# Layer 0 of a four-layer hybrid on one core: the step size and C are kept by chunk in memory, and the sums of the four directions are added there

## The chip, the core and the metric

One core of a Trainium2 chip runs the whole network in one launch. Its engines run side by side, each through its own list of instructions in order: TensorE (PE, with its weight loads shown as PEld), VectorE (DVE), ScalarE (ACT), GpSimd (POOL) and SyncE (SP, which here only issues transfers). They wait for each other through semaphores. The metric is the device time of one execution in microseconds, as the median of repeated runs.

## The reference

The input is 4 images of 64 x 64 positions with 128 channels. The change touches layer 0 alone, a selective scan over 256 inner channels and 16 states, in four directions (along rows, along columns, and both backwards):

```python
xz = x @ w_in
xc, z = jnp.split(xz, 2, axis=-1)
xc = conv_general_dilated(xc, conv_w, ...) + conv_b          # 3 x 3, by channel
xa = jax.nn.silu(xc)
x_flat = xa.reshape(b, L, D_INNER)                           # L = 4096
dts, Bp, Cp = jnp.split(x_flat @ w_xproj, [DT_RANK, DT_RANK + D_STATE], axis=-1)
dts = dts @ w_dt
xs = jnp.stack([x_flat, x_t, jnp.flip(x_flat, 1), jnp.flip(x_t, 1)], axis=1)

def step(h, inp):                                            # 4096 steps, every direction
    u_i, d_i, b_i, c_i = inp                                 # d_i = softplus(dts + b_dt)
    dA = jnp.exp(d_i[..., None] * A)
    h = h * dA + (d_i * u_i)[..., None] * b_i[:, None, :]
    y = jnp.einsum('gdn,gn->gd', h, c_i)
    return (h, y)

y = (the four directions, each put back in place, added) + 4 * xa * D
y = layer_norm(y) * silu(z);   x = x + y @ w_out
```

delta, B and C are the same in all four directions: they follow the scan's own time, and only u differs. Layers 1 to 3 are not changed.

## The kernel before

**Units and iterations.** A unit is one image b and one half h of the 256 channels. A unit is 64 chunks c of 64 time steps, so layer 0 is one loop of 4 x 2 x 64 = 512 iterations, I = (2b + h) * 64 + c. An iteration handles the four directions of its chunk as two pairs: kp = 0 along rows (forward j = 0, backward j = 1) and kp = 1 along columns. Partitions hold 64 channels (or times) for two groups of states; 16 states are two groups of 8.

**What an iteration does**, with lines of the profile:

- `fetch` (SP) loads for iteration I + 2: C broadcast over partitions (`ct`, L570), u of the four directions with time on partitions (`xo`, L583), and, for h = 1, the diagonals of B (`dg`, L588). `load` loads delta for four chunks (`dl` L536, `dp` L539).
- `start` copies delta's chunk backwards (`dlr`, ACT, L599); `diagonal` makes diagonals of B (ACT, L608, 16 instructions, h = 0 only) and stores them (L611); `decay` makes exp(delta A) for the next four chunks (ACT, L560).
- `delta` turns delta's chunk so that time stands on partitions, forwards in one half and backwards in the other (PE, L617, into the PSUM tile `aux`); `inputs` multiplies it with u into `du`, two DVE instructions (L628), one for each pair.
- `products`: PE multiplies du with the diagonals (L637) and so makes delta u B with channels on partitions again, in PSUM.
- `scan`: for each direction DVE adds the state carried over into the first column (L650) and scans 1024 columns (L653). POOL then makes the carry for the next chunk (`cy`, L661) and multiplies the states by C in place (`big`, L669, one for each pair).
- `total`: PE adds the 8 states of a group and both groups (L682, 16 matmuls in two parts). In the second half of a unit (c >= 32) the four places of `yr` and `yc` hold the sums of the opposite direction, and PE adds these in by identity matmuls (L694). ACT copies the sums into `yr` (rows) or `yc` (columns), L701. Both tiles are whole (128 x 4096) and single. yr is stored by SP (L706) in the second half, yc is added to y0 in memory by a POOL transfer (L710) at the end of a unit.

**Order.** PE, DVE and ACT run in the order written out in the loop; Tile's scheduler places POOL's and SP's instructions. In iteration I the loop writes: start(I + 1), diagonal(I + 1), products(I, 0), scan(I, 0), total(I - 2, 1), a side step, decay, products(I, 1), delta(I + 1), inputs(I + 1), scan(I, 1), a side step, total(I - 1, 0). The states lie in three buffers, the products' PSUM in three.

**Side steps.** A generator `beside` is advanced twice an iteration, one step each time, from c = 4 of h = 0 on. For image 0 it runs `spectra` (tables for layer 1, lines 814 to 872), for later ones `back` of the image before: y = yr + y0 (POOL, L468), layer norm (L475 to L497), the product with silu(z) (POOL, L501), w_out (L508, L512) and the store. Then `front` of the next image (group norm, w_in: L281, L328) and, from h = 1 on, `middle`: convolution (L369), silu, turning of u into memory `xT` (L387, L391), w_xproj (L402), B turned (L417), and softplus for both halves (ACT L435 to L440, DVE L442 to L446) with delta stored to `dl`. front and middle of image 0 run ahead of the loop, back of the last image after it.

Of the kernel before, what the change touches and what calls it, by code (L numbers as in the profile page):

```python
# [14 lines left out]
P = 128  # L15
# [144 lines left out]
def layer0(cm, x, W, x1, also, kept):  # L160
# [5 lines left out]
    with ExitStack() as ctx:  # L166
# [4 lines left out]
        t4 = ctx.enter_context(tc.tile_pool(name="l0t4", bufs=4))  # L171
        p2 = ctx.enter_context(tc.tile_pool(name="l0p2", bufs=2))
# [32 lines left out]

        both = tl(wp, [P, TC], "both")
# [27 lines left out]

        yr = tl(wp, [P, S], "yr")
        yc = tl(wp, [P, S], "yc")

        aux = tl(pp, [P, 2, 2, P], "aux")
        yp = aux[:, 0].rearrange("p k (j t) -> p k j t", t=TC)
        pt2 = aux[:, 1]  # L240
# [19 lines left out]
        def begin(b):  # L260
            img[b] = {
                "zs": tl(dr, [P, 2, S], "zs"),
                "dl": tl(dr, [2, P, S], "dl_d"),
                "ct": tl(dr, [NST, S], "ct_d"),
                "xT": tl(dr, [2, S, P], "xT_d"),
                "y0": tl(dr, [P, 2, S], "y0_d"),
                "yr": tl(dr, [P, 2, S], "yr_d"),
            }
# [77 lines left out]
        def shifted(i, pool, tag):  # L346

            k, h = divmod(i, 2)
            x3 = tl(pool, [3 * CG, 4, 8 * PADW], tag, bufs=None if tag == "big" else 1)
            for dy in range(3):  # L350
                s0 = (8 * k + dy) * PADW
                nc.sync.dma_start(
                    x3[dy * CG : (dy + 1) * CG],
                    xc_d[4 * h : 4 * h + 4, :, s0 : s0 + 8 * PADW].rearrange("g p s -> p g s"),
                )
            return x3

        def middle(b, bank, pool, tag, ahead):

            ready = [shifted(i, pool, tag) for i in range(ahead)]  # L360
            for k in range(NBLK):
                cols = slice(k * BLK, (k + 1) * BLK)
                xa = []
                for h in range(2):
                    ps = bank()
                    x3 = ready.pop(0)
                    for dx in range(3):
                        for g in range(4):
                            nc.tensor.matmul(  # L369
                                ps[g * CG : (g + 1) * CG, :], lhsT=cdiag[:, 4 * h + g, dx, :],  # L370
                                rhs=x3[:, g, 0 : 8 * PADW].rearrange(
                                    "p (r w) -> p r w", w=PADW
                                )[:, :, dx : dx + HW],
                                start=(dx == 0), stop=(dx == 2),
                            )
                    if 2 * k + h + ahead < 2 * NBLK:
                        ready.append(shifted(2 * k + h + ahead, pool, tag))
                    xh = tl(tmp, [P, BLK], "t2k")
                    nc.scalar.activation(xh, ps, AF.Silu, bias=vec[:, 0, h : h + 1])
                    y0 = tl(tmp, [P, BLK], "t2k")  # L380
                    nc.scalar.activation(y0, xh, AF.Copy, scale=d4[:, h : h + 1])
                    nc.sync.dma_start(img[b]["y0"][:, h, cols], y0)
                    xa.append(xh)
                    yield
                    ps = bank()
                    for i in range(4):
                        nc.tensor.transpose(  # L387
                            ps[:, i * P : (i + 1) * P], xa[h][:, i * P : (i + 1) * P], cm.ident
                        )
                    t = tl(tmp, [P, 4, P], "t2k")  # L390
                    nc.scalar.copy(t, ps.rearrange("p (t c) -> p t c", c=P))  # L391
                    nc.sync.dma_start(
                        img[b]["xT"][h, cols, :].rearrange("(t p) c -> p t c", p=P), t
                    )
                    yield
                    if h == 0:
                        yield
                        yield
# [12 lines left out]
                nc.sync.dma_start(img[b]["ct"][:, cols], xd[RANK + NST : n, :])  # L411
# [10 lines left out]
                nc.vector.tensor_copy(BT[:, 8 * k : 8 * k + 8, :], pb)  # L422
                for h in range(2):
# [23 lines left out]
                    nc.sync.dma_start(img[b]["dl"][h, :, cols], r)  # L447
                yield

# [81 lines left out]
        def load(q):  # L531

            b, h, c = place(q * QC)
            cols = slice(c * TC, (c + QC) * TC)
            dl = tl(p2, [P, QC * TC], "dl")
            nc.sync.dma_start(dl, img[b]["dl"][h, :, cols])  # L536
            dp = tl(p2, [P, 2, QC, TC], "dp")
            for p in range(2):
                nc.sync.dma_start(  # L539
                    dp[p * TC : (p + 1) * TC].rearrange("p g c t -> p g (c t)"),  # L540
                    img[b]["dl"][h, :, cols].rearrange("(g d) t -> d g t", d=TC),
                )
            return {"dl": dl, "dp": dp, "dA": dA[q % 2], "h": h}
# [21 lines left out]
        def fetch(I):  # L565
# [3 lines left out]
            for p in range(2):  # L569
                nc.sync.dma_start(  # L570
                    ct[p * TC : (p + 1) * TC],
                    img[b]["ct"][p * NH0 : (p + 1) * NH0, c * TC : (c + 1) * TC]
                    .unsqueeze(0).to_broadcast([TC, NH0, TC]),
                )
            xo = tl(p2, [P, 2, P], "xo", bufs=3)
            xT = img[b]["xT"][h]
# [12 lines left out]
            inp[I] = {"ct": ct, "xo": xo, "dg": dg}  # L589
# [4 lines left out]
        def start(I):  # L594
            b, h, c = place(I)
            q = {"c": c, "h": h, "w": quads[I // QC], **inp.pop(I)}
            dlc = q["w"]["dl"][:, c % QC * TC : (c % QC + 1) * TC]
            dlr = tl(p2, [P, TC], "dlr")
            nc.scalar.copy(dlr, dlc[:, ::-1])  # L599
            q["dl"] = dlc, dlr  # L600
            return q
# [11 lines left out]
        def delta(q):  # L613

            pt = pt2[:, q["c"] % 2]
            for j in range(2):
                nc.tensor.matmul(  # L617
                    pt[j * TC : (j + 1) * TC, :], lhsT=q["dl"][j], rhs=cm.ident,
                    start=True, stop=True,
                )  # L620
            q["pt"] = pt

        def inputs(q):

            q["du"] = []
            for kp in range(2):
                d_ = tl(p2, [P, P], f"du{kp}")
                nc.vector.tensor_tensor(d_, q["xo"][:, kp, :], q["pt"], ALU.mult)  # L628
                q["du"].append(d_)

        def products(q, kp):
            bs = [tl(db, [P, 2 * NH0, TC], "db") for _ in range(2)]
            for g in range(2):
                for j in range(2):
                    half = slice(j * TC, (j + 1) * TC)
                    for p in range(2):
                        nc.tensor.matmul(  # L637
                            bs[j][p * TC : (p + 1) * TC, g * NH0 : (g + 1) * NH0, :],
                            lhsT=q["du"][kp][half, g * TC : (g + 1) * TC],
# [5 lines left out]
        def scan(I, q, kp, bs, st, old, new):  # L645
            c = q["c"]
            for j in range(2):
# [11 lines left out]
            us = slice(2 * kp, 2 * kp + 2)  # L659
# [16 lines left out]
        def total(I, part):  # L676
            b, h, c = place(I)
            st = states[I]
            late = c >= NCHUNK // 2
            for n in range(4 * part, 4 * part + 4):  # L680
                for p in range(2):
                    nc.tensor.matmul(  # L682
                        yp[p * TC : (p + 1) * TC], lhsT=both,
                        rhs=st[:, :, p * NH0 + n, :], start=(n == 0),
                        stop=(n == NH0 - 1 and not late),
                    )
            if part == 0:
                return
            vs = [views(yc if kp else yr, c)[2 * j + kp] for j in range(2) for kp in range(2)]
            for j in range(2 if late else 0):  # L690

                for kp in range(2):
                    v = vs[2 * j + kp]
                    nc.tensor.matmul(  # L694
                        yp[:, kp, j, :], lhsT=cm.ident, rhs=v[:, ::-1] if j else v,
                        start=False, stop=(j + kp == 2),
                    )
# [5 lines left out]
            if late and c % 8 == 7:  # L703
                for r in (c - 7, NCHUNK - 1 - c):
                    rows = slice(r * TC, (r + 8) * TC)
                    nc.sync.dma_start(img[b]["yr"][:, h, rows], yr[:, rows])  # L706
            if c == NCHUNK - 1:
                for r in range(2):
                    rows = slice(r * S // 2, (r + 1) * S // 2)
                    nc.gpsimd.dma_start(  # L710
                        img[b]["y0"][:, h, rows], yc[:, rows], accum_op=ALU.add
# [12 lines left out]
        for _ in run(front(0, turn_bank), middle(0, turn_bank, big, "big", 2)):  # L724
            pass
        N = 2 * B * NCHUNK
        states, quads, inp = {}, {0: load(0), 1: load(1)}, {}
# [9 lines left out]
        delta(nxt)  # L737
# [10 lines left out]
        with tc.manual_schedule(engines=engines):  # L748
            for I in range(N):
                b, h, c = place(I)  # L750
                clock[0] = I
                if h == 0 and c == 4:
                    gens = [back(b - 1, own_bank) if b else also(
                        tl(p2, [P, 4, 8 * PADW], "x3", bufs=1)[:, 0, 0 : 4 * C], tmp, t4, own_bank
                    )]
                    if b + 1 < B:
                        gens += [
                            front(b + 1, own_bank), wait(I - c + NCHUNK),
                            middle(b + 1, own_bank, p2, "x3", 1),
# [22 lines left out]
                if I > 1:  # L782
                    total(I - 2, 1)
# [10 lines left out]
                if nxt:  # L794
                    delta(nxt)
# [4 lines left out]
                if I:  # L800
                    total(I - 1, 0)
                carry = new
            total(N - 2, 1)
            total(N - 1, 0)
            total(N - 1, 1)
# [4 lines left out]
def spectra(cm, W, cst, sp_d, room, tmp, t4, bank):  # L810

    nc = cm.nc
    kern = room.rearrange("p (a c) -> p a c", c=C)
# [1504 lines left out]
```

## Time and profile before

| | |
|---|---|
| median of 3 runs | 11002.33 us (10992.38 to 11011.69) |
| the profiled execution, time and span | 10974.05 us and 10972.3 us |
| busy over the span: PE, DVE, ACT, POOL | 86%, 69%, 49%, 49% |
| the 512 iterations (first to last scan) | 281.7 to 6370.9 us |
| units of h = 0 (b = 0 to 3) | 762.9, 810.7, 807.2, 790.8 us |
| units of h = 1 (b = 0 to 3) | 747.2, 746.1, 750.4, 673.9 us |
| granted TensorE clock in the units | 0.92 to 0.99 |

A group line reads: line, engine, operation, out<-in, shapes, count | busy us, mean ns of one | idle time of the engine just before them, and what ended most of it. A waits line reads: who waited <- for whom: total us, times, longest. A timeline line reads: start us, duration us, engine, line, operation, out<-in, shapes, how many merged, and in brackets the idle time before it and its releaser. The third table row and the unit rows come from one answer of the windows view.

### The profile page before, as it was taken

What the parts mean: (1) busy time and instruction counts of PE and PEld (TensorE: products, weight loads), DVE (VectorE), ACT (ScalarE), POOL (GpSimd) and SP (SyncE); (2) the same over time, 40 slices, a digit from 0 to 9 for tenths busy, and PEclk for the clock granted to TensorE, in tenths of its full rate; (3) what the DMA queues carried; (4) which work ended last, traced back from release to release, by engine and by line L of the source; (5) the groups of instructions that cost most, each with busy time, mean ns of one, the idle gap of its engine ahead of it and who ended that gap; (6) DMA issues with size and microseconds to landing.
All of it is one profiled execution on the core that took longest, in us unless ns stands there. A gap on an engine that the chain in (4) does not pass through costs nothing. (4 is left out here: it accounts for less than half of the span.)

```text
span 10972.3 us, 163387 instructions
## 1 busy us (share of the span) xinstructions
PE 9474.1 (86%) x59368; PEld 4529.1 (41%) x59368; DVE 7569.2 (69%) x11174; ACT 5425.1 (49%) x13536; POOL 5331.9 (49%) x2581
## 2 busy tenths in 40 slices
PE   6789998889998899998889954999999956988886
PEld 2344444344443344443344432444444434544442
DVE  1898988888988898988899966545452122355546
ACT  6666543555544564545542223777776622433321
POOL 0788888878888888887889940000000000000000
PEclk7899999999999899998999977999999976677777
DMA  5334443334443334443333341111100065022101
GB/s 147 106 107 149 131 128 114 109 109 149 136 132 116 107 117 151 135 122 113 109 106 99 103 120 36 41 35 35 39 24 17 16 191 104 17 46 56 37 24 46
DMA packets 1471160, 1009.46 MB, mean 92 GB/s; under 512 B 697540, under 2 KB 1296296, under 8 KB 1466008
## 3 DMA queue, kind: packets, MB, share of 16 engines
q1 hardware_dynamic: 1468056, 982.24, 30.3%
q0 software_dynamic: 2304, 16.78, 0.7%
q8 instruction: 475, 7.78, 0.3%
q14 instruction: 325, 2.66, 0.1%
HBM read 667.01 MB, written 331.61 MB: 91 GB/s over the span
## 5 line engine op out<-in xcount | busy, mean ns | idle before, releaser
L653 DVE TENSOR_TENSOR_SCAN big<-dA,db 128x1024 f32<-128x1024 f32 x2048 | 4680.0, 2286 | 82.1 <-ACT dA L560 3.2
L669 POOL TENSOR_TENSOR big<-big,ct 128x2048 f32<-128x2048 f32 x1024 | 4646.1, 4537 | 85.0 <-DVE big L653 5.4
L637 PE MATMUL db<-dg,du 64*64 64x512 f32 x16384 | 2442.7, 617 | 101.1 <-DVE db L650 87.8
L682 PE MATMUL aux<-big,both 128*64 128x256 f32 x16384 | 2104.0, 401 | 407.1 <-DVE db L650 260.6
L682 PEld LDWEIGHTS aux<-big,both 128*64 128x64 f32 x16384 | 1202.8, 142 | 1396.1 <-issue 622.9
L701 ACT COPY yr<-aux 128x64 f32<-128x64 f32 x1024 | 226.6, 222 | 2668.6 <-PE aux L694 1250.7
L637 PEld LDWEIGHTS db<-dg,du 64*64 64x64 f32 x16384 | 748.2, 135 | 1321.2 <-issue 1218.4
L608 ACT ACTIVATE dg<-mask,BT 128x64 f32<-128x64 f32 x4096 | 1007.4, 341 | 4.0 <-DMA dg_d<-dg 4.0
L1441 PE MATMUL av<-e,x 128*128 128x512 f32 x2048 | 974.0, 592 | 4.6 <-ACT e L1436 4.6
L1392 PE MATMUL qk<-a,xT 128*128 128x512 f32 x2048 | 966.6, 594 | 8.6 <-ACT e L1396 7.8
L1396 ACT ACTIVATE e<-qk,nk 128x512 f32<-128x512 f32 x1024 | 692.9, 685 | 539.2 <-PE qk L1392 538.4
L560 ACT ACTIVATE dA<-dp,A 128x252 f32<-128x252 f32 x2048 | 870.5, 509 | 1.4
L971 POOL TENSOR_TENSOR g_rs<-g_rs,qrow 128x4 f32<-128x4 f32 x32 | 41.1, 1285 | 1499.9 <-DVE g_rs L970 1499.9
L661 POOL TENSOR_TENSOR cy<-big,a 128x32 f32<-128x32 f32 x1008 | 272.8, 271 | 821.7 <-DVE big L653 524.4
L1392 PEld LDWEIGHTS qk<-a,xT 128*128 128x128 f32 x2048 | 378.0, 190 | 462.3 <-issue 358.0
L1441 PEld LDWEIGHTS av<-e,x 128*128 128x128 f32 x2048 | 381.6, 190 | 434.7 <-issue 393.6
L1436 ACT ACTIVATE e<-e 128x1024 f32<-128x1024 f32 x510 | 538.7, 1056 | 15.3
L1917 ACT ACTIVATE e<-s 72x576 f32<-72x576 f32 x448 | 273.3, 642 | 492.0 <-PE s L1910 489.0
L628 DVE TENSOR_TENSOR du<-xo,aux 128x128 f32<-128x128 f32 x1024 | 248.2, 284 | 379.5 <-PE aux L617 286.2
L650 DVE TENSOR_TENSOR db<-db,cy 128x16 f32<-128x16 f32 x2016 | 336.9, 167 | 202.0 <-PE db L637 184.2
L1928 POOL COPY vp<-vt 72x160 f32<-72x160 f32 x56 | 19.6, 352 | 890.8 <-PE po L1934 874.4
L2150 DVE SCALAR_TENSOR_TENSOR tex<-x,gw,tex 128x128 f32<-128x128 f32 x768 | 264.5, 344 | 256.1 <-PE x L2144 241.2
(525 smaller groups left out, 10869.4 us busy)
## 6 DMA issues: line engine op xcount, KB each, us to landing
ct<-ct_d SPq DMA_DIRECT2D x1024, 128.0 KB
dg_d<-dg SPq DMA_DIRECT2D x256, 512.0 KB
dg<-dg_d SPq DMA_DIRECT2D x256, 512.0 KB
xo<-xT_d SPq DMA_DIRECT2D x2048, 32.0 KB
x<-xc_d SPq DMA_DIRECT2D x144, 264.0 KB
dp<-dl_d SPq DMA_DIRECT2D x256, 128.0 KB
t2k<-in_x SPq DMA_DIRECT2D x96, 256.0 KB
sp<-sp_d SPq DMA_DIRECT2D x16, 1280.0 KB
```

The lines of the kernel that those rows point to most:

```text
L560: nc.scalar.activation(w["dA"][:, :, g, n, 1:], w["dp"][:, g, :, 1:], AF.Exp, scale=A[:, w["h"], g, n : n + 1],)
L608: nc.scalar.activation(q["dg"][:, n, :], mask, AF.Copy, scale=BT[:, q["c"], n : n + 1])
L637: nc.tensor.matmul(bs[j][p * TC : (p + 1) * TC, g * NH0 : (g + 1) * NH0, :], lhsT=q["du"][kp][half, g * TC : (g + 1) * TC], rhs=q["dg"][ha ...
L650: nc.vector.tensor_tensor(bs[j][:, :, 0], bs[j][:, :, 0], old[:, u, :], ALU.add)
L653: nc.vector.tensor_tensor_scan(st[:, u].rearrange("p n t -> p (n t)"), q["w"]["dA"][:, c % QC].rearrange("p g n t -> p (g n t)"), bs[j].re ...
L669: nc.gpsimd.tensor_tensor(sv, sv, q["ct"].rearrange("p n t -> p (n t)").unsqueeze(1) .to_broadcast([P, 4, NH0 * TC]), ALU.mult,)
L682: nc.tensor.matmul(yp[p * TC : (p + 1) * TC], lhsT=both, rhs=st[:, :, p * NH0 + n, :], start=(n == 0), stop=(n == NH0 - 1 and not late),)
L1392: nc.tensor.matmul(ps, lhsT=me["xT"][:, kt * P : (kt + 1) * P], rhs=me["a"][k], start=True, stop=True,)
L1396: nc.scalar.activation(e[:, j, :], ps, AF.Exp, bias=me["nk"][:, kt : kt + 1], scale=2.0)
L1436: nc.scalar.activation(es[g + 2], es[g + 2], AF.Exp)
L1441: nc.tensor.matmul(avs[b, k], lhsT=img[b]["x"][:, kt, :], rhs=e[:, j, :], start=(kt == 0), stop=(kt == NT - 1),)
L1917: nc.scalar.activation(e.rearrange("p j h q -> p j (h q)"), ss[p][0:HALF, :, 0 : 2 * WIN], AF.Exp, scale=0.5,)
```

## The change

- middle: once softplus is done for both halves, delta is turned (PE, then ACT), its halves reversed by a matmul with `flip`, copied again and stored in memory by chunk (`dT`): eight stores a block of 512 positions. C is stored by chunk, so that a chunk's eight states lie in one piece.
- The loop loads the turned delta (`dt`) in fetch, and `du` becomes one DVE instruction over both pairs. delta(), dlr and the dl load go.
- The sums go into tiles of 8 chunks (`yr0`, `yr1`) and of half a unit (`yc`), two of each. The identity matmuls go. yr is stored by SP in a unit's first half and added in memory by POOL transfers in its second; yc is added in memory twice a unit.
- Both parts of total work on I - 2: part 0 after scan(I, 0), part 1 at the end. A third side step is taken at c % 4 == 2 of h = 0; beside starts at c = 5; the idle steps in middle go. The convolution's input is loaded in two halves from the pool of `t4k` tiles, and spectra's kernels lie in `padded[0]`.

```diff
+        flip = tl(wp, [P, P], "flip")
+        nc.vector.memset(flip, 0.0)
+        for p in range(2):
+            half = slice(p * TC, (p + 1) * TC)
+            nc.vector.tensor_copy(flip[half, half], cm.ident[half, half][:, ::-1])
...
-        yr = tl(wp, [P, S], "yr")
-        yc = tl(wp, [P, S], "yc")
...
-                "ct": tl(dr, [NST, S], "ct_d"),
+                "ct": tl(dr, [NCHUNK, NST, TC], "ct_d"),
+                "dT": tl(dr, [2, NCHUNK, 2, TC, P], "dT_d"),
...
-            x3 = tl(pool, [3 * CG, 4, 8 * PADW], tag, bufs=None if tag == "big" else 1)
+            x3 = [tl(pool, [3 * CG, 2, 8 * PADW], tag) for _ in range(2)]
...
-                    if h == 0:
-                        yield
-                        yield
...
                     nc.sync.dma_start(img[b]["dl"][h, :, cols], r)
-                yield
+                    rs.append(r)
+
+                yield
+                for h in range(2):
+                    t = None
+                    for j in range(2):
+                        ps = bank()
+                        if j == 0:
+                            for i in range(4):
+                                nc.tensor.transpose(
+                                    ps[:, i * P : (i + 1) * P], rs[h][:, i * P : (i + 1) * P],
+                                    cm.ident,
+                                )
+                        else:
+                            nc.tensor.matmul(
+                                ps, lhsT=flip, rhs=t.rearrange("p t c -> p (t c)"),
+                                start=True, stop=True,
+                            )
+                        t = tl(tmp, [P, 4, P], "t2k")
+                        nc.scalar.copy(t, ps.rearrange("p (t c) -> p t c", c=P))
+                        for i in range(2):
+                            nc.sync.dma_start(
+                                img[b]["dT"][h, 8 * k + i : 8 * k + 8 : 2, j]
+                                .rearrange("t r c -> r t c"), t[i * TC : (i + 1) * TC],
+                            )
+                        yield
...
+            dt = tl(p2, [P, P], "dt", bufs=3)
+            nc.sync.dma_start(dt, img[b]["dT"][h, c].rearrange("j r c -> (j r) c"))
...
         def inputs(q):
 
-            q["du"] = []
-            for kp in range(2):
-                d_ = tl(p2, [P, P], f"du{kp}")
-                nc.vector.tensor_tensor(d_, q["xo"][:, kp, :], q["pt"], ALU.mult)
-                q["du"].append(d_)
+            q["du"] = tl(p2, [P, 2, P], "du")
+            nc.vector.tensor_tensor(
+                q["du"], q["xo"], q["dt"].unsqueeze(1).to_broadcast([P, 2, P]), ALU.mult
+            )
...
+                if c % 8 == 0:
+                    for i in range(2):
+                        ys[i] = tl(yb, [P, 8 * TC], f"yr{i}")
+                if c % (NCHUNK // 2) == 0:
+                    ys[2] = tl(yb, [P, HW, TC], "yc")
...
-            for j in range(2 if late else 0):
-
-                for kp in range(2):
-                    v = vs[2 * j + kp]
-                    nc.tensor.matmul(
-                        yp[:, kp, j, :], lhsT=cm.ident, rhs=v[:, ::-1] if j else v,
-                        start=False, stop=(j + kp == 2),
-                    )
...
+                for i, r0 in enumerate((c - 7, NCHUNK - 1 - c)):
+                    to = img[b]["yr"][:, h, r0 * TC : (r0 + 8) * TC]
+                    if c < NCHUNK // 2:
+                        nc.sync.dma_start(to, ys[i])
+                    else:
+                        nc.gpsimd.dma_start(to, ys[i], accum_op=ALU.add)
-            if c == NCHUNK - 1:
+            if c % (NCHUNK // 2) == NCHUNK // 2 - 1:
                 for r in range(2):
                     rows = slice(r * S // 2, (r + 1) * S // 2)
                     nc.gpsimd.dma_start(
-                        img[b]["y0"][:, h, rows], yc[:, rows], accum_op=ALU.add
+                        img[b]["y0"][:, h, rows],
+                        ys[2].rearrange("p r w -> p (r w)")[:, rows], accum_op=ALU.add,
                     )
...
-                if h == 0 and c == 4:
+                if h == 0 and c == 5:
...
                 scan(I, now, 0, bs, st, carry, new)
                 if I > 1:
-                    total(I - 2, 1)
+                    total(I - 2, 0)
                 if beside:
                     next(beside, None)
...
                 bs = products(now, 1)
                 if nxt:
-                    delta(nxt)
                     inputs(nxt)
                 scan(I, now, 1, bs, st, carry, new)
                 if beside:
                     next(beside, None)
-                if I:
-                    total(I - 1, 0)
+                if I > 1:
+                    total(I - 2, 1)
+                if beside and h == 0 and c % 4 == 2:
+                    next(beside, None)
                 carry = new
```

## The prediction

> **What bounds the kernel now.** I read first the page's digits in 40 slices and its list of costliest groups. Layer 0 takes the first 23 slices, and there DVE, PE and POOL are all busy eight or nine tenths. The first two groups are the scan on DVE and the product with C on POOL:
>
> ```profile
> L653 DVE TENSOR_TENSOR_SCAN big<-dA,db 128x1024 f32<-128x1024 f32 x2048 | 4680.0, 2286 | 82.1 <-ACT dA L560 3.2
> L669 POOL TENSOR_TENSOR big<-big,ct 128x2048 f32<-128x2048 f32 x1024 | 4646.1, 4537 | 85.0 <-DVE big L653 5.4
> ...
> L628 DVE TENSOR_TENSOR du<-xo,aux 128x128 f32<-128x128 f32 x1024 | 248.2, 284 | 379.5 <-PE aux L617 286.2
> L650 DVE TENSOR_TENSOR db<-db,cy 128x16 f32<-128x16 f32 x2016 | 336.9, 167 | 202.0 <-PE db L637 184.2
> ```
>
> Second, the windows by unit (64 iterations). The 512 iterations run from 281.7 to 6370.9 us: 6089.2, of which DVE is busy 5422.5, PE 5445.6, POOL 5073.8 and ACT 3063.3. So DVE idles 667, and the two rows above say before what: du waits for TensorE's turned delta, and the carry (L650) for the products.
>
> Third, the waits view of that window, for causes:
>
> ```profile
> POOL cy L661 <- DVE big L653: 524.4, 342, 17.6
> DVE du L628 <- PE aux L617: 286.2, 265, 15.1
> ...
> DVE db L650 <- PE db L637: 184.2, 62, 17.9
> ...
> POOL t4k L468 <- DMA t4k<-yr_d: 80.4, 15, 10.4
> ACT yr L701 <- DMA yr_d<-yr: 69.7, 6, 21.0
> ```
>
> POOL waits for DVE, so DVE leads; the last row is the single yr tile that is still being stored when the next unit writes it.
>
> Fourth, the timeline of a plain iteration (start, duration):
>
> ```profile
> 6013.84 2.29 DVE L653 TENSOR_TENSOR_SCAN big<-dA,db 128x1024 f32<-128x1024 f32 x1
> ...
> 6016.24 0.27 POOL L661 TENSOR_TENSOR cy<-big,a 128x32 f32<-128x32 f32 x1
> 6016.28 0.48 DVE L628 TENSOR_TENSOR du<-xo,aux 128x128 f32<-128x128 f32 x2 [0.15 <-DMA xo<-xT_d]
> ...
> 6016.59 4.53 POOL L669 TENSOR_TENSOR big<-big,ct 128x2048 f32<-128x2048 f32 x1
> 6016.68 0.18 DVE L650 TENSOR_TENSOR db<-db,cy 128x16 f32<-128x16 f32 x1
> 6016.89 2.29 DVE L653 TENSOR_TENSOR_SCAN big<-dA,db 128x1024 f32<-128x1024 f32 x1
> ```
>
> Scan follows scan after 2.40 us, but after 3.05 with du between: du costs 0.65, and the iteration 10.25.
>
> Fifth, a long stall of the output part (back), and a DVE instruction that met POOL:
>
> ```profile
> 2227.46 2.34 POOL L468 TENSOR_TENSOR t4k<-t4k 128x1024 f32<-128x1024 f32 x1 [6.49 <-PE aux L617]
> ...
> 2234.65 3.68 PE L682 MATMUL aux<-big,both 128*64 128x256 f32 x16 [7.36 <-POOL big L669]
> ...
> 2241.22 0.18 DVE L650 TENSOR_TENSOR db<-db,cy 128x16 f32<-128x16 f32 x1 [6.26 <-PE db L637]
> ```
>
> ```profile
> 481.70 4.51 POOL L669 TENSOR_TENSOR big<-big,ct 128x2048 f32<-128x2048 f32 x1
> 482.95 3.54 DVE L862 SCALAR_TENSOR_TENSOR t4k<-t4k 128x256 f32<-128x256 f32 x1
> 486.41 0.17 DVE L650 TENSOR_TENSOR db<-db,cy 128x16 f32<-128x16 f32 x1
> ```
>
> The first: POOL is late by one add, the sums of iteration I-1 wait for it, the products stand behind them on PE, and DVE pays 6.3. The second: L862 reads two SBUF tiles, starts 1.25 into a POOL product and ends 0.28 after it, 3.54 us for what L856, of the same size, does in 0.42 (median).
>
> **What DVE must still do.** du becomes one instruction of 256 columns from two SBUF tiles. Nearest row: L856, 0.40 us, the next instruction 0.32 later (521.25 to 521.57). I take 0.33 for 0.65. 512 x (4 x 2.40 + 0.33) = 5084. The side work on DVE in the loop is unchanged: reciprocals 94, softplus 99, back 77 (L480, L494, L512), spectra's other four 41 (L856, L862, L865, L868), statistics and copies 26, together 338 with rounding. Together 5422.
>
> **What goes from the waits.** du no longer follows TensorE, so the 286 us, and most of the other 93 before L628, go: PE drops the turning (0.45 us an iteration) and, in late iterations, four identity adds (0.8). Sums of I-2 instead of I-1 give POOL half an iteration more, so the 6.3 us stalls of back go. Double yr and yc tiles take the wait at c = 2 away. The copy dlr (0.24 of ACT each) and the dl load go; both were off the path.
>
> **What stays or comes**, in us:
> - The wait for spectra's kernels at 372.95 (17.9) and the first scan's 3.2: 21, untouched.
> - Start of back, three images. Iterations c = 2 and 4 took 24.1 and 19.1, that is 23 above plain. POOL's add still waits for y0 and yr, now both accumulated by POOL's DMA (14.2 to landing), but the carries alone then hold DVE: 11 each, 33. Bounds 0 and 69.
> - A convolution step is 2.78 on PE (133.6/48). With products and sums, 1.95 each, its half takes 6.7 against DVE's 4.8; PE is some 1.5 ahead: 0.4 x 48 = 19. Bounds 0 and 1.9 each (91).
> - The input part (front) puts 1.0 of PE into a step (four of 105.7/96 and one of 31.6/48, by five), at 2.25 steps an iteration with the third ones: 7.8 + 2.3 = 10.1 against 9.93. Some 78 iterations (30 of image 0, 24 each of 1 and 2, counted in the program's order) x 0.3 = 23; bounds 0 and 70.
> - du against POOL. POOL's pair cy and product repeats every 4.82, two make 9.65, with the a0 products (0.5 in four iterations) and du's hold (cy took 0.40 behind L856 at 388.38, 0.27 elsewhere) about 9.9. So du arrives when POOL's product is just ending. In iterations without DVE side work 0.2 x 290 = 58. What makes POOL later is no longer absorbed but paid at the next du: 24 adds L468 of 2.35, 55; 48 pairs of accumulating DMAs instead of 8 (1.76 a pair at 1811.49), of which DVE's side work hides a third, 55. In all 168. Lower bound nothing, if a tensor_tensor isn't held; upper bound half a product at each du, 2.27 x 512 = 1162. I take 168 because the rate of POOL (9.9) and DVE (9.93) keeps du at the product's end.
> - SP gains a dt load an iteration (xo's loads take 0.6 each), dT stores and twice as many convolution loads. In the plain iteration above it issues for 1.28 (ct), 0.57 (dg) and 5.84 (xo), 7.7 of 10.25, and loads are 1.5 iterations ahead: 15 for late ones (xo cost 22.4 so far). Bounds 0 and 45.
>
> Together 279; the loop becomes 5701, 388 less.
>
> The turns themselves in the loop (48 x 2 halves: four transposes 0.66, a 512-column matmul 1.1, two copies 0.58) lie in steps of their own on PE and ACT, under DVE. The third steps, the dropped idle ones and the start at c = 5 only place them; x3 in halves from another pool and the kernels' new room move buffers. I count nothing for these; uncovered, a turn step is a PE step of 1.1, less than a convolution's 2.8.
>
> **Before the loop** they are not hidden. In the program's order PE turns all of a block's delta before the next block's convolution, which now runs beside the softplus. From the last logarithm: three DVE steps 2.1, transposes 0.7, copy 0.6, flip 1.1, convolution 4.0, latencies 0.3, in all 8.8 to the next silu, against 1.3 now (152.37 to 153.68). 7 x 7.5, and at the end 4.5 (four copies 2.3 and their waits for PE), make 57. Bounds: 32 copies alone, 19, and 80. **After it** two more accumulating DMAs stand ahead of y0's: 4.
>
> Net -388 + 57 + 4 = -327. The profiled execution took 10974.05 (span 10972.3), 28 below the median of 11002.33: 10647 there, 10675 as a median.
>
> **Two rules.** The Trainium skill (SBUF — State Buffer, "Who interferes with whom") speaks against the change: a VectorE instruction with two SBUF inputs is held for a whole GpSimd instruction that reads SBUF, tensor_tensor included, and one with a PSUM input, as du is now, is not. The row here is of another operation (L862), and L856 met only a product's last 0.2 us; by the rule du pays the lock, by those short rows alone the sum would be 168 lower. The Trainium skill (DMA: Bandwidth & Descriptors, "Specifications") wants at least 512 B a descriptor; C's packets go from 256 B to 2 KB. By that rule transfers gain; by the rows (DMA share 0.33 to 0.46 in the loop, 22.4 us of waits for xo) almost nothing, and I count nothing.
>
> **The rivals.**
> - Slower: du meets POOL's products in the middle. For it: L862, held eight times out of eight. Against: after one hold the two are in step. It costs 2.27 x 512 = 1162 for 168: about 11670. It decides from 0.97 us a du, (327 + 168)/512, on; I count 0.33. Chance 0.13.
> - TensorE becomes the bound: waits move from du to the products. For it: PE is 5446 of 6089 busy. Against: it loses 0.45 to 1.25 an iteration. Half of 286 comes back (143), and convolution and front reach half their upper bounds (27 + 12): 10857. Chance 0.2.
> - No lock at all for this operation: 10507. Chance 0.17.
> - The forecast, 10675: 0.5.
>
> The range 10530 to 10900 takes in the forecast with most of its bounds, the TensorE case and half of the third; it leaves out the slower one. The three lower cases make faster 0.83 with 0.04 taken off for no change (within 0.2%, about what a measurement can tell), slower 0.13.
>
> **What would show it.** Right: du to du 9.95 to 10.15 in plain iterations of the last unit; no wait of ACT for yr's store and none of du for PE; the loop starts near 340 and lasts near 5700; du's mean between 0.4 and 0.9. Wrong: du's mean above 1.3 (the lock), long waits of the carry for the products (TensorE), or a loop that starts past 365.

## The result and the profile after

The changed kernel takes 10981.89 us (median of 12 runs, 10969.18 to 11011.92), the kernel before 11000.39 (12 runs, 10985.66 to 11015.72): a ratio of 0.9986, interval 0.9977 to 0.9995. That is 0.14% faster, within the 0.2% that the prediction called no change. The forecast was 10675, and its range began at 10530 and ended at 10900: it was wrong by 307 us. The profiled execution took 10973.7, its span 10971.9; the forecast had 10647 there, and the 327 us between them are what the steps below nearly add up to.

All of the miss lies in the loop. It starts at 339.7 us (forecast near 340), and the stretch behind it grew by 2.3 (forecast 4). But the loop lasts 6028.5 instead of the forecast 5701; it was 6089.2 before.

The page's list of costliest groups shows which wait went and what came (busy us, mean ns of one, then the idle time before the group and what ended it):

```profile
L668 DVE TENSOR_TENSOR_SCAN big<-dA,db 128x1024 f32<-128x1024 f32 x2048 | 4679.5, 2286 | 83.7 <-PE db L651 5.2
L683 POOL TENSOR_TENSOR big<-big,ct 128x2048 f32<-128x2048 f32 x1024 | 4654.8, 4546 | 78.6 <-DVE big L668 0.2
...
L641 DVE TENSOR_TENSOR du<-xo,dt 128x256 f32<-128x256 f32 x512 | 537.9, 1051 | 12.7 <-DMA xo<-xT_d 12.7
...
L665 DVE TENSOR_TENSOR db<-db,cy 128x16 f32<-128x16 f32 x2016 | 333.7, 166 | 238.2 <-PE db L651 219.0
```

Scan and product are as they were. In front of du hardly any idle time is left (379.5 before), and none of it waits for TensorE: as forecast. But du itself takes 1.05 us on average, where 0.33 of work and 0.33 of hold were forecast, and the carry (L665) still waits 219 us for the products (184.2 before).

The waits view of the loop, 340 to 6368 us (sum, times, longest):

```profile
POOL cy L675 <- DVE big L668: 343.4, 215, 12.0
POOL cy L675 <- DVE db L665: 337.2, 216, 13.4
DVE db L665 <- PE db L651: 219.0, 135, 13.6
...
POOL t4k L498 <- DMA t4k<-yr_d: 40.6, 13, 8.2
...
DVE db L665 <- POOL cy L675: 16.9, 5, 6.3
```

POOL still waits for DVE. The wait for the stored yr tile (69.7 before) is gone, and the output part's wait for yr's load is half of the 80.4 before.

A plain iteration of the last unit, from the timeline (start, duration, DVE and POOL rows):

```profile
6012.92 0.52 DVE L641 TENSOR_TENSOR du<-xo,dt 128x256 f32<-128x256 f32 x1
6013.12 0.44 POOL L675 TENSOR_TENSOR cy<-big,a 128x32 f32<-128x32 f32 x1
6013.36 0.17 DVE L665 TENSOR_TENSOR db<-db,cy 128x16 f32<-128x16 f32 x1
...
6013.64 4.54 POOL L683 TENSOR_TENSOR big<-big,ct 128x2048 f32<-128x2048 f32 x1
...
6022.97 0.52 DVE L641 TENSOR_TENSOR du<-xo,dt 128x256 f32<-128x256 f32 x1
```

From du to du it is 10.05 us, in the forecast's 9.95 to 10.15. So plain iterations are as predicted; the loss must lie in iterations that have other work.

The windows view gives it away. It shows the busy time of du's line alone in the three units that hold a convolution and a softplus (b0h1, b1h1, b2h1; columns: stretch, length, busy us and count, clock, DMA share, GB/s):

```profile
1103.00:1809.00 706.00, 35.83 (x64) 0.98 0.55 154
2623.00:3373.00 750.00, 76.88 (x64) 0.95 0.53 148
4181.00:4934.00 753.00, 74.74 (x64) 0.95 0.53 147
```

The three do the same work. In the first, du costs 35.8, in the others twice as much, and these are 44 and 47 us longer. Here is one softplus of b0h1, then one of b1h1, from the timeline:

```profile
1161.45 2.29 DVE L668 TENSOR_TENSOR_SCAN big<-dA,db 128x1024 f32<-128x1024 f32 x1
1163.65 0.67 DVE L447 SCALAR_TENSOR_TENSOR bg<-bg,t2k 128x512 f32<-128x512 f32 x1
1163.82 0.26 POOL L675 TENSOR_TENSOR cy<-big,a 128x32 f32<-128x32 f32 x1 [3.78 <-DVE big L668]
1164.16 4.53 POOL L683 TENSOR_TENSOR big<-big,ct 128x2048 f32<-128x2048 f32 x1
1164.36 0.70 DVE L450 TENSOR_TENSOR bg<-t2k,bg 128x512 f32<-128x512 f32 x1
1165.09 0.69 DVE L451 TENSOR_TENSOR t2k<-bg,t2k 128x512 f32<-128x512 f32 x1
...
1168.30 2.29 DVE L668 TENSOR_TENSOR_SCAN big<-dA,db 128x1024 f32<-128x1024 f32 x1
...
1170.51 0.40 DVE L641 TENSOR_TENSOR du<-xo,dt 128x256 f32<-128x256 f32 x1
```

```profile
2702.52 0.67 DVE L447 SCALAR_TENSOR_TENSOR bg<-bg,t2k 128x512 f32<-128x512 f32 x1
...
2703.23 0.70 DVE L450 TENSOR_TENSOR bg<-t2k,bg 128x512 f32<-128x512 f32 x1
2703.45 4.53 POOL L683 TENSOR_TENSOR big<-big,ct 128x2048 f32<-128x2048 f32 x1
2703.96 0.69 DVE L451 TENSOR_TENSOR t2k<-bg,t2k 128x512 f32<-128x512 f32 x1
2704.57 3.70 DVE L641 TENSOR_TENSOR du<-xo,dt 128x256 f32<-128x256 f32 x1
```

An iteration has two places for side steps: behind the first pair of scans, where du stands too, and behind the second. In b0h1 the softplus has the second place, and du comes straight after a scan. In b1h1 it has the first, between scan and du. The scans let POOL start its next product at 2703.45, the softplus keeps DVE until 2704.6, and du, arriving 1.1 us into the product, is held until 0.29 after its end.

Counted over the loop by what stands ahead of du on DVE: 403 du follow a scan and take 278.7 us, 108 follow side work and take 258.7, 2.4 us each. Set against 0.398, the mean of a du that is never held (below), the first lose 118 and the second 216. Of the 118, 81 fall on 38 du that met a late POOL; the other 365 lose 0.1 each. In 98 of the 101 du over 1 us a product is under way, and du ends 0.279 to 0.293 us after it; in the other three it is an add of the output part (L498).

### The profile page after: what moved, and what is told of

Read it like the earlier page. It is cut to its first block, busy times and chain, and to the rows that moved or that the text cites. A ratio compares the mean times of both kernels' runs of the same rounds, so it can differ in the third digit from the quotient of the medians.

```text
span 10971.9 us, 156222 instructions
## 1 busy us (share of the span) xinstructions
PE 9481.5 (86%) x55656; PEld 4193.0 (38%) x55656; DVE 7830.4 (71%) x10665; ACT 5425.3 (49%) x13151; POOL 5452.3 (50%) x2661
## 5 line engine op out<-in xcount | busy, mean ns | idle before, releaser
L651 PE MATMUL db<-dg,du 64*64 64x512 f32 x16384 | 2771.2, 639 | 411.1 <-DVE db L665 377.6
L703 PE MATMUL yp<-big,both 128*64 128x256 f32 x16384 | 2160.5, 408 | 73.3 <-ACT yc L717 68.0
L703 PEld LDWEIGHTS yp<-big,both 128*64 128x64 f32 x16384 | 1163.2, 145 | 1404.2 <-issue 840.2
L717 ACT COPY yr<-yp 128x64 f32<-128x64 f32 x1024 | 225.2, 220 | 1646.6 <-PE yp L703 1644.7
L675 POOL TENSOR_TENSOR cy<-big,a 128x32 f32<-128x32 f32 x1008 | 347.8, 345 | 705.7 <-DVE big L668 343.4
L641 DVE TENSOR_TENSOR du<-xo,dt 128x256 f32<-128x256 f32 x512 | 537.9, 1051 | 12.7 <-DMA xo<-xT_d 12.7
L665 DVE TENSOR_TENSOR db<-db,cy 128x16 f32<-128x16 f32 x2016 | 333.7, 166 | 238.2 <-PE db L651 219.0
L1948 POOL COPY vp<-vt 72x160 f32<-72x160 f32 x56 | 19.7, 352 | 899.3 <-PE po L1954 896.4
```

The source lines that it names most:

```text
L641: nc.vector.tensor_tensor(q["du"], q["xo"], q["dt"].unsqueeze(1).to_broadcast([P, 2, P]), ALU.mult)
L651: nc.tensor.matmul(bs[j][p * TC : (p + 1) * TC, g * NH0 : (g + 1) * NH0, :], lhsT=q["du"][half, kp, g * TC : (g + 1) * TC], rhs=q["dg"][ha ...
L703: nc.tensor.matmul(yp[p * TC : (p + 1) * TC], lhsT=both, rhs=st[:, :, p * NH0 + n, :], start=(n == 0), stop=(n == NH0 - 1),)
```

## The experiments

The theory (A) was that du is held where DVE's side work stands ahead of it; the rival (B) that TensorE, with the third steps and the turns, would set the pace anyhow. Unless named otherwise, an edit is to the changed kernel. Loop starts of the same instructions differ by 12 us between sets of runs (339.7 and 351.7), so smaller differences of the start are not read. The kernel before, run again with each set, had medians of 10984 to 11000; so a difference between runs of different sets is good to some 16 us.

**du ahead of the side step.**

```diff
                     total(I - 2, 0)
+                if nxt:
+                    inputs(nxt)
                 if beside:
                     next(beside, None)
...
                 bs = products(now, 1)
-                if nxt:
-                    inputs(nxt)
```

> Changed kernel, with one edit: du of the next iteration is issued on DVE straight after the first pair of scans, ahead of the side step that stands there, instead of behind it. Nothing else moves. Theory A (held behind side work): the 101 du over 1 us, which make most of du's 537.9 us, are those before which DVE did side work, so that POOL had begun its next product; now du comes while POOL is only starting the carry. du's sum falls to 230-280 us (mean 0.45-0.55), the loop from 6028.5 to 5700-5800, the time from 10982 to 10690-10760. Theory B (TensorE): the third steps and the turn steps make TensorE late anyway, and a du that is held only takes the place of that wait; du's sum falls as well, but the carry's waits for the products grow from 219 us by 200 or more, and the time stays above 10920.

Measured: 10831.15, ratio 0.9859 (0.9831 to 0.9888). The group of du on the page:

```profile
L641 DVE TENSOR_TENSOR du<-xo,dt 128x256 f32<-128x256 f32 x512 | 354.5, 692 | 12.7 <-DMA xo<-xT_d 12.7
```

183 us less of du, 150 less of time, and the carry's waits for the products stay at 218: against B, for A in direction. The size was missed (10690 to 10760 expected): du still loses 151 us. Of it, 114 fall on 52 du that are still over 1 us: at 14 of them POOL had just issued accumulating transfers, at 4 an add of the output part stood there; why POOL was late at the other 34 is open.

**delta in PSUM.** ACT copies the tile that was loaded; du's order stays.

```diff
+            q["pt"] = pt2[:, c % 2]
+            nc.scalar.copy(q["pt"], q["dt"])
...
-                q["du"], q["xo"], q["dt"].unsqueeze(1).to_broadcast([P, 2, P]), ALU.mult
+                q["du"], q["xo"], q["pt"].unsqueeze(1).to_broadcast([P, 2, P]), ALU.mult
```

> Changed kernel, with one edit: ACT copies the delta tile into PSUM (128x128, one more ACT instruction an iteration), and du reads it there; du stays behind the side step. Theory A: with one input in PSUM du isn't held at all, so that its mean is 0.35-0.50 us, none is over 1 us, and the time is 10680-10760, within 40 of the kernel with du issued first. If the hold comes from the wait of something else than the SBUF port (a late xo or delta tile), du stays near 1 us here. Theory B: the time stays above 10920, with the carry's waits for the products above 400 us.

Measured: 10613.08, ratio 0.9658 (0.9632 to 0.9685), better than expected. Its groups by line on DVE (busy us, mean ns, idle before and all that ended it):

```profile
L670 DVE TENSOR_TENSOR db<-db,cy 128x16 f32<-128x16 f32 x2016 | 336.0, 167 | 217.3 <-PE db L656 180.8 <-POOL cy L680 31.5 <-POOL big L688 2.0
...
L646 DVE TENSOR_TENSOR du<-xo,aux 128x256 f32<-128x256 f32 x512 | 203.8, 398 | 26.4 <-DMA ct<-ct_d 12.7 <-DMA xo<-xT_d 12.6 <-ACT dg L638 1.0
```

The same instruction at the same place, with the same companions, takes 0.398 us on average and never over 0.45 once one input lies in PSUM. The loop is 5685.6 instead of 6028.5: 343 less, of which 334 are du's. This settles that du was held by POOL, and did not wait for a late tile.

**One idle step.** No instruction is added or altered; the softplus of two units moves to the other place.

```diff
             ready = [shifted(i, pool, tag) for i in range(ahead)]
+            if b > 1:
+                yield
             for k in range(NBLK):
```

> Changed kernel, with one edit: the middle part of images 2 and 3 begins with one idle step, so that every later step of it takes the other of an iteration's two places. No instruction is added, dropped or altered. In the program's order 24 of 64 du then no longer stand behind softplus work of DVE in each of the units b1h1 and b2h1 (none is left, as in b0h1 now); all other units keep theirs. Theory A (held behind side work): these two units fall from 750 and 753 to 705-715 us, their du sums from 77 and 75 to below 42, the time by 70-95 to 10890-10915. Theory B (TensorE's load, or the softplus itself, sets the length): the units stay above 740 and the time within 20 of 10982.

Measured: 10916.99, ratio 0.9919 (0.9896 to 0.9943). du's line in b0h1, b1h1 and b2h1, from the windows view:

```profile
1121.00:1826.00 705.00, 37.55 (x64) 0.98 0.54 154
2636.00:3345.00 709.00, 34.65 (x64) 0.98 0.54 156
4157.00:4863.00 706.00, 35.03 (x64) 0.99 0.55 157
```

Units and du sums came where expected, the time a little above. With this, the place of the side work is shown to be the cause of the 44 and 47 us of these units, by itself.

**delta turned by TensorE again**, all other parts of the change kept (one du of 256 columns from PSUM; the turn ahead of the sums of I-2).

```diff
                 scan(I, now, 0, bs, st, carry, new)
+                if nxt:
+                    delta(nxt)
                 if I > 1:
                     total(I - 2, 0)
...
-                (turns of delta into memory, dT stores, dt loads; empty steps in their place)
```

> Changed kernel with its first part undone: delta is not turned into memory; the dl load, the reversed copy on ACT and the turning matmuls of TensorE are back (issued ahead of the sums of I-2), du is one instruction of 256 with delta in PSUM; all else (C by chunk, sums in memory, formed later, third steps) stays. Theory A: no hold and no turns before the loop, so the loop starts near 282 as before the change, du's mean is 0.35-0.50, and the time is 10620-10720: nearly all that the forecast had, from the other parts alone. Theory B: TensorE has 0.45 us more in each iteration and stays the bound; the time is 10850-10950.

Measured: 10587.99, ratio 0.9642 (0.9616 to 0.9668), better than expected. B falls: TensorE has more to do (38,090 matmuls in the loop instead of 36,338) and nothing is lost by it. Turning delta into memory, with its hold and its start, costs 3.4% against leaving it to TensorE (0.9986 to 0.9642).

**The same, without third steps** and with the idle steps of before.

```diff
-                if beside and h == 0 and c % 4 == 2:
-                    next(beside, None)
...
-                for _ in range(5):
-                    yield
+                yield
```

> The kernel with delta turned by TensorE, without the third steps and the empty steps in place of the turns, idle steps as before the change. If third steps crowd TensorE (the carry's waits for the products, 176 us there), those waits fall to 100-140 and the time falls by 30-80 to 10510-10560. If placing costs nothing, as the forecast had it, the time is 10570-10610. Slower (above 10610) if steps now run into the last iterations of a unit and are drained at once.

Measured: 10468.87, ratio 0.9524 (0.9508 to 0.954), below the expected range, and the best of all. The carry's group:

```profile
L656 DVE TENSOR_TENSOR db<-db,cy 128x16 f32<-128x16 f32 x2016 | 335.4, 166 | 153.4 <-PE db L642 117.4
```

Its waits for the products fall from 176.1 to 117.4, and the loop by 95 us, from 5675 to 5580. Of these, 52 lie in b0h1, b1h1 and b2h1 (700, 705, 708 to 687 each), which never had third steps. So it is where steps fall, idle ones included, that costs; third and idle steps were not taken apart.

**The same, and du ahead of the side step** (the edit of the first experiment).

> The kernel with delta turned by TensorE and no third steps (0.9524 of before), with du issued ahead of the side step. du has PSUM there, so nothing is held; what can change is only that TensorE's products get du earlier in the 46 iterations of the input and output units in which side work stood before it. Theory A: 46 x 0.5-1.0, the time falls by 10-40 to 10430-10460. If those products were waiting for other things: within 10 of 10469.

Measured: 10552.2, ratio 0.9593 (0.9576 to 0.9611): 83 slower, where a gain was expected. The timeline of DVE, and that of POOL, at the input part's statistics:

```profile
2352.28 0.40 DVE L632 TENSOR_TENSOR du<-xo,aux 128x256 f32<-128x256 f32 x1
2352.59 0.15 DVE L298 COPY gn_s<-bg 128x1 f32<-128x1 f32 x1
2352.77 0.16 DVE L300 TENSOR_TENSOR gn_d<-gn_mv,gn_s 128x1 f32<-128x1 f32 x1
2352.97 4.42 DVE L301 SCALAR_TENSOR_TENSOR gn_d<-gn_d,gn_mv 128x1 f32<-128x1 f32 x1
```

```profile
2352.88 4.49 POOL L674 TENSOR_TENSOR big<-big,ct 128x2048 f32<-128x2048 f32 x1 [0.18 <-POOL cy L666]
```

du can't be held here, but it pushed the side work back by 0.4 us, into the product. An instruction of one column, 0.22 us elsewhere, takes 4.42. Of spectra's eight L877 (0.67 each before), four take 4.7 to 5.1. The unit b0h0 alone is 30 us longer. The hold had found other instructions. But that is the smaller part of it. DVE's busy time in the loop grew by 17 us only, as another of spectra's groups (L874) was held less. Its waits for TensorE grew by 51: the carry's for the products from 117.4 to 149.1, and du's from 0.4 to 19.7.

```profile
L656 DVE TENSOR_TENSOR db<-db,cy 128x16 f32<-128x16 f32 x2016 | 335.2, 166 | 181.9 <-PE db L642 149.1 <-POOL cy L666 31.4
...
L632 DVE TENSOR_TENSOR du<-xo,aux 128x256 f32<-128x256 f32 x512 | 202.9, 396 | 22.5 <-PE aux L694 19.7 <-DMA ct<-ct_d 2.8
```

Together these make up the loop's 70 us; the stretch behind the loop, which the edit does not touch, was 32 longer in this profiled execution. Why TensorE came later was not found.

**The output side alone**: as the best kernel, but with C's old layout (its edit is below) and du as two instructions.

```diff
-            q["du"] = tl(p2, [P, 2, P], "du")
...
+            for kp in range(2):
+                d_ = tl(p2, [P, P], f"du{kp}")
+                nc.vector.tensor_tensor(d_, q["xo"][:, kp, :], q["pt"], ALU.mult)
```

> The kernel before with the output side of the change alone: row and column tiles doubled and small, both halves added in memory, sums of I-2 instead of I-1, and with that TensorE's turning of delta issued ahead of the sums (between the two halves of a sum it can't stand), convolution inputs in halves. Left as before: delta turned by TensorE, du as two instructions with delta in PSUM, C's layout, no third steps. If this side carries the gain (theory A of the kernel with delta turned by TensorE, 0.9642 of before), the ratio is 0.965-0.975: du's wait for TensorE below 40 us, no wait for the yr store, back's stalls of 6 us gone; du's two instructions cost 0.25 more an iteration, 60-130 us. If it were the single du that brings the gain, the ratio is above 0.985.

Measured: 10631.02, ratio 0.9675 (0.9655 to 0.9694), as expected. Doubled tiles, sums in memory, later sums, the earlier turn and the convolution's input in halves bring 359 us together. DVE's wait for TensorE before du, 286.2 before, is 0.3. The carry still waits 185.5 for the products and 76.5 for POOL.

**C's old layout**, first with delta turned by TensorE (third steps in), then in the changed kernel.

```diff
-                    ct[p * TC : (p + 1) * TC].rearrange("p n t -> p (n t)"),
-                    img[b]["ct"][c, p * NH0 : (p + 1) * NH0, :].rearrange("n t -> (n t)")
+                    ct[p * TC : (p + 1) * TC],
+                    img[b]["ct"][p * NH0 : (p + 1) * NH0, c * TC : (c + 1) * TC]
```

> The kernel with delta turned by TensorE, with C's old layout in memory (256 B pieces instead of 2 KB). The forecast counted nothing for the layout: time within 15 of 10588, DVE's waits for C, xo or the delta diagonals below 15 us. If the small pieces slow the queue (SP's issue or the transfers), waits for ct and xo rise and the time is 10620 or more.

> Changed kernel with C's old layout (256 B pieces). In the kernel with delta turned by TensorE the old layout cost 177 us, as late loads, stores and accumulations. If that comes from the queue, which has more to do in the changed kernel than before (delta's stores and loads, halves of the convolution's inputs), it costs 100-250 here too: 11080-11230, slower than before the change. If DVE's held du hide the late loads, it costs below 60.

Measured: 10765.28 (0.9783, 0.9762 to 0.9805), 177 slower than with the new layout (155 by the ratios to the kernel before, as the two ran in different sets); and 11178.12 (1.0169, 1.0149 to 1.0189), 196 slower (201 by the ratios). The forecast counted nothing here. The waits views, first of the new layout, then of the old one (both with delta turned by TensorE):

```profile
DVE db L654 <- PE db L640: 176.1, 143, 5.1
...
POOL t4k L472 <- DMA t4k<-yr_d: 42.9, 12, 8.1
...
DVE db L654 <- POOL cy L664: 35.3, 9, 9.4
```

```profile
DVE db L651 <- PE db L637: 280.8, 182, 8.5
...
POOL t4k L469 <- DMA t4k<-yr_d: 131.2, 22, 13.9
...
DVE db L651 <- POOL cy L661: 86.3, 22, 15.2
...
PE db L637 <- DMA dg<-dg_d: 27.5, 10, 6.8
```

C is read by POOL, which hardly waits for it in the first case (5.5 us in the loop); in the second it waits 43.7, of which 33.7 at the loop's first carry, where the kernel before waits 21.0. But in the first case the output part's add on POOL waits 88 us longer for yr, and the carry 105 longer for the products and 51 longer for POOL. A part of the products' lateness can be seen: their matmuls idle for the diagonals of B, 27.5 us in the first case and 78.2 in the second, against 0.4 at most with the new layout. The pages count 455,168 packets more with the old layout (1,485,739 against 1,030,571, for the same bytes). That these slow the other transfers is inferred from the two, and by what way is open: the DMA engines are busy 0.44 of the loop with either layout. The cost is measured.

**Image 0's turns** one block later, ahead of the second convolution, copies on DVE (with du first); then spread over the next block in quarters (with delta in PSUM).

```diff
+                    if b == 0 and h == 0 and k:
+                        yield from turns(k - 1, rs)
...
+                if b or k == NBLK - 1:
+                    yield from turns(k, rs)
```

```diff
+                late = iter(()) if b or not k else turns(
+                    k - 1, rs, [own_bank, own_bank, bank, own_bank], nc.vector.tensor_copy
+                )
...
+                    for _ in range(h + 1):
+                        next(late, None)
...
+                next(late, None)
```

> The kernel with du issued first, and image 0's turns of delta placed one block later, behind the first convolution of the next block, with their copies on DVE (idle there) instead of ACT. The forecast's reading of the start (turns of a block stand between the softplus and the next convolution, 7 x 7.5 + 4.5 = 57 us; measured 58) expects the loop to start at 285-305 instead of 339.7, and the time to be 35-55 below the kernel with du issued first: 10640-10720. If the 58 us came from ACT's copies or from the queue instead, the start stays above 320.

> The kernel with delta copied to PSUM, with image 0's turns of a block spread over the next block, one quarter at a time (behind the first transposition, two behind the second, one behind the projection), copies on DVE, a bank of their own. With the turns all ahead of the second convolution the start fell by 10 of 58 only. If the cost is that four dependent quarters stand in one place on TensorE, the loop now starts near 300-315 instead of 351 and the time is 10560-10580; if it is something else (the tiles, the queue), the start stays above 335 and the time above 10600.

Measured: 10829.97 (0.9858, 0.9832 to 0.9885) and 10608.03 (0.9648, 0.9632 to 0.9664), each equal to its base (0.9859 and 0.9658). The starts, 341.7 and 332.9 against 351.7 and 351.3, are hardly beyond the 12 us between sets. Both expectations failed: the 58 us are not won back by moving the turns. A part of it may be a queue. In the changed kernel's timeline SP issues delta's stores ahead of the first loads of the loop:

```profile
323.04 5.60 SPq L474 DMA_DIRECT2D dT_d<-t2k  x7
...
328.69 0.62 SPq L567 DMA_DIRECT2D dp<-dl_d  x1
329.36 1.26 SPq L598 DMA_DIRECT2D ct<-ct_d  x2
```

What holds the blocks before that, once the turns are spread, was not found.

## Why the prediction was wrong, step by step

- **Before and after the loop**: right in size. 58.0 for 57, 2.3 for 4. By the silu of each block's second half (84.5 to 303.5 us, against 83.9 to 258.5 before) a block grew by 6.3 where 7.5 was counted; what follows the last block grew by 13 for 4.5, with SP's stores above in it. That moving the turns would win it back did not hold, so the reason that was given for the size is not shown.
- **du's wait for TensorE, the yr store, DVE's own work**: right. The last comes out at 5425 (6028.5 less holds and waits) for 5422.
- **du against POOL, the first step that failed**: counted 168, measured 334. (Its own sum is loose: 24 adds of 2.35 are 56, and 40 more pairs at 1.76, two thirds of them paid, are 47, so that it gives 161.) The step said that du arrives when the product is just ending, and it counted the end of the hold only in the 290 iterations without side work on DVE. Most du behind a scan do arrive so, and with those that met a late POOL they lose 118, less than was counted. But side work stands between the scans and du in 108 iterations. It lets POOL begin the next product first, so that each such du loses 2.0 on average, 216 together. The rule that was weighed beside it (the Trainium skill, SBUF — State Buffer, "Who interferes with whom") also says that issue order decides who blocks; the prediction used only its other half, that two SBUF inputs are held. The runs agree with both halves: 0.398 us with an input in PSUM, 4.42 for one column without; and a loss of 0.3 for du that follow the scan, 2.0 for du that come behind side work. The prediction's own sign of the lock, a mean above 1.3, did not show: the mean was 1.05.
- **TensorE, front, convolution, start of back, late loads, the second step that failed**: 111 counted, some 269 measured: 224 of DVE waiting for products, 17 for POOL's carry, 28 of side work waiting for TensorE. In the three convolution units alone the products cost 77 where 19 was taken (its upper bound was 91). Placing was counted at nothing; without third steps and with idle steps back, 95 us of loop went. What made the rest of the 158 is open. A rival that no run tests is TensorE's clock: the granted clock was 0.93 in this loop, against 0.95 before and 0.96 to 0.97 with delta in PSUM and with delta turned by TensorE; a matmul of the products took 639 ns on average instead of 617 before. Either miss alone would have stayed inside the range (10833 with the 158, 10841 with the 166 of the hold); together they left it.
- **C's layout**: counted at nothing. The kernel before, with the small pieces, had few late loads in its loop (80.4 us of POOL's waits for yr, 22.4 of du's for xo); in the changed kernel the pieces would have made it 1.7% slower than before. That kernel gives the engines delta's stores and loads and the accumulations as well; but as the kernel without delta's transfers pays about as much, these are not needed for it. The Trainium skill (DMA: Bandwidth & Descriptors, "Specifications") wants at least 512 B a transfer for line rate. The 177 and 196 us speak for that rule and against the rows that were used, waits of a lighter queue.
- **The rivals**: "slower by the lock at mid-product" had the mechanism and the wrong number of cases: 63 of the 108 du behind side work were held for over 1 us, not all 512. Of "TensorE becomes the bound", priced at 182, some 128 came (224 of waits for 96); it isn't what took du's gain, for those waits stayed at 218 when the holds were cut by half. "No lock at all" (10507) is what PSUM gives, and came to 10613.

From the best version to the changed kernel it is 0.9524 to 0.9986, some 508 us. Holds (334), start (58) and placing (95), each from its own pair of runs, make 487 of them: that is what turning delta into memory and the steps it needs cost, and it used up all that the rest of the change brought.

## What to carry to other kernels

Where an instruction can be held by another engine's, ask not how often the two meet in the steady loop, but what stands between the event that starts the other engine and that instruction. One input in PSUM, even by an extra copy on an engine with time to spare, ended the question here for that instruction. After any shift, look again for which instruction now comes first behind the other engine's start. And price a layout by the queue as it will be with the change, not by the waits of the queue before.

## What was not expected of the hardware

- A DVE instruction of 128x1 took 4.42 us instead of 0.22, held for a whole POOL product; the length of the hold has nothing to do with the size of what is held.
- A held du of 256 columns ended 0.279 to 0.293 us after the product's end (98 cases). With delta turned by TensorE and du first, held instructions of one column ended 0.02 after it, and of 512 columns 0.55. What comes after the product grows with the width, so the hold itself seems to end with the product.
- C in pieces of 256 B instead of 2 KB, 455,168 packets more for the same bytes, cost 177 and 196 us, in the first case while POOL waited 5.5 us for the data they carried.
